# The first heads' 1x1 convolution by patch rows, in quarters of TensorE, with the first head's depthwise convolution two steps behind it

## The chip, the core and the metric

The kernel runs on one core of one Trainium2 chip. The metric is the device time of one execution in microseconds (us), the median of several runs. Engines: TensorE (matrix products; in the profile PE, its weight loads PEld), VectorE (DVE), ScalarE (ACT), GpSimd (POOL) and SyncE (SP), which issues most DMAs.

## What is computed

The input x has 48 channels of 256x256 in float32. Layer 0 is an attention over image patches, layer 1 a product along width, height and channels in windows of 64; both act on a group norm (16 groups of three channels) and are added to their input.

```python
# layer 0, on g = group norm of x
qkv = einsum('bchw,oc->bohw', g, w_qkv)          # 1x1 convolution, 48 -> 144 channels
qkv = dwconv3x3(qkv, w_dw)                       # depthwise 3x3, zero border
q, k, v = split(qkv, 3)                          # then patches of 4x4, 8 heads of 96 x 4096
q, k = l2norm(q), l2norm(k)                      # over the 96 values of a patch and head
attn = softmax(einsum('bhcn,bhcm->bhnm', q, k) * temperature)
out = fold(einsum('bhcn,bhnm->bhcm', v, attn))
x = x + einsum('bchw,oc->bohw', out, w_proj)
# layer 1, on the group norm of the new x
x = x + sum_t einsum('bchw,wW,hH,cC->bCHW', windows of 64, Ws[t], Hs[t], Cs[t])
```

## The kernel before

**Reading x (L403 to L423).** `xr` holds the whole image, its upper and lower 128 rows as two halves of 48 partitions (96 in all). Ten parts per half are loaded, one half through SyncE's queue, the other through ScalarE's; VectorE takes statistics of every two rows (L422), and `group_stats` turns them into a mean and a factor per channel. These go into the weights: `wq` (heads 0 and 1, a block per half) and `wr` (heads 2 to 7) are scaled (L425, L426), and `bias` is made of the means. The weights themselves are 35 small loads on GpSimd's queue (L87 to L112, `dwt` the last 21 of them); the row of zeros `zr` (L407), which borders the DRAM copies, is cleared by GpSimd too.

**The 1x1 convolution of heads 0 and 1 (L469 to L478, `pointwise`).** For each two rows of both halves one matmul (96 partitions in, 72 out, 512 columns) fills one of four PSUM buffers, which ScalarE (L156) and VectorE (L154) empty in turn into `ot0`, four buffers of eight rows. Each is stored into the DRAM tensor `t1[0]`. Heads 2 to 7 follow during the attention, in `Strip`, two rows at a time with half of the array for each half of the image (L177).

**The depthwise convolution (`Depthwise`).** A head's 64 patch rows (four pixel rows each) lie in seven chunks of nine. Step r treats patch row r of all seven chunks at once: 3 x 7 x 6 = 126 partitions (q, k and v; chunk; channel), each with a `pad` of six rows of 258 pixels, the four of the patch row and one on either side. Ten steps cover the head (the tenth is patch row 63). `load` reads `pad` from DRAM with three DMAs; the nine taps are either `first` on ScalarE and eight `tap`s on VectorE (L228), or 18 matmuls against diagonal matrices on TensorE (`taps_on_tensor`, L217). Then follow `square` (ScalarE, L239), `reduce` (VectorE, L243), `norm` (TensorE, L247, adds up over a head's channels), `root` and `scale` (VectorE), `patches` (ScalarE, L279, sorts pixels by patch), `high` and `low` (the split into two parts, L285 and L289), and three stores into `qkv`.

**Head 0 (`depthwise_first`).** Steps 0, 2, 4, 6, 8 and 9 have their taps on TensorE, 1, 3, 5 and 7 on VectorE. The order of TensorE's instructions is that of the program text (`manual_schedule`): taps of step 0, taps of step 2, norms of steps 0 and 1, taps of step 4, norms of 2 and 3, and so on. The other engines' instructions, and the DMA queues', are put in order by the framework's planner, which goes by the program text as far as an instruction is ready by its own costs; each engine then runs its list strictly in order. Every load of a `pad` waits for the stores of the rows that it reads.

**After that** a branch on the temperature (L494, a barrier between all engines; its body does not run here), then the keys are loaded and the attention over eight heads starts, during which the depthwise convolutions of the next head run step by step. Projection and layer 1 end the kernel.

## Time and profile before

| what | us |
|---|---|
| median of 3 runs (lowest, highest) | 3679.08 (3667.85, 3684.79) |
| profiled execution | 3676.93 |
| its span, first to last instruction | 3674.8 |
| TensorE busy in the span | 3466.3 |
| VectorE, ScalarE, GpSimd busy | 2138.7, 1872.6, 541.8 |
| last statistics of x end | 68.97 |
| first, last matmul of the 1x1 convolution | 73.8, 132.5 |
| first taps on TensorE | 147.26 |
| last norm of head 0 | 249.9 |
| queries of head 0 are loaded from | 267.6 |
| attention's logits run without waiting from | 287.2 |

Times in the profile count from the first instruction. "Busy" is the time in which an engine executes an instruction; a float32 matmul leaves two records of half its work each. "PEclk" is the clock that TensorE was granted as a share of the full one, and "DMA share" the busy share of the core's 16 DMA engines. In a timeline a line gives start, length, engine, line of the kernel, operation, what is written from what is read, the count, and in brackets the idle time before it with what ended that.

### The profile page before, as it was taken

Reading aid. Unit: us, or ns where it says so; the run is one execution under the profiler, and the core shown is the slowest. Engines: PE = TensorE matmul, PEld = TensorE weight load, DVE = VectorE, ACT = ScalarE, POOL = GpSimd, SP = SyncE. Lnnn points to the kernel's source line nnn. Section 1 sums busy time; section 2 is a strip of 40 time slices with the busy share of each in tenths; the row PEclk is TensorE's granted clock in tenths of the full one; section 3 lists DMA queues with packets and bytes.
Section 4 is the critical chain, followed back from the end, with each engine's and each line's share of the span. In section 5 each row is a group of like instructions: output and inputs, shape, how many; then the busy total and the mean of one; then the engine's idle time right before and its main releaser. Section 6 shows DMA issues by size and latency. Waiting matters only on the chain.

```text
span 3674.8 us, 100335 instructions
## 1 busy us (share of the span) xinstructions
PE 3466.3 (94%) x44252; PEld 2908.2 (79%) x44252; DVE 2138.7 (58%) x3514; ACT 1872.6 (51%) x2747; POOL 541.8 (15%) x628
## 2 busy tenths in 40 slices
PE   2869999999999999999999999999999999965998
PEld 1337777888989888888899988888899888833776
DVE  5454674179628962895389439934993222267654
ACT  0235676566646654665466556655664444400332
POOL 2030111012211211121112112211221100010011
PEclk9989999999999999999999999999999999976999
DMA  7455666533323332333233323332333220089774
GB/s 161 154 131 151 172 173 167 159 96 93 92 70 84 97 93 80 81 93 86 80 81 93 94 76 86 87 93 71 94 85 87 65 53 19 15 213 234 120 137 93
DMA packets 275299, 386.49 MB, mean 105 GB/s; under 512 B 77298, under 2 KB 211810, under 8 KB 270920
## 3 DMA queue, kind: packets, MB, share of 16 engines
q1 hardware_dynamic: 235942, 264.95, 27.4%
q0 software_dynamic: 35424, 106.40, 12.7%
q10 hardware_dynamic: 3490, 8.64, 1.1%
q8 instruction: 350, 5.73, 0.7%
q14 instruction: 93, 0.76, 0.1%
HBM read 234.76 MB, written 144.90 MB: 103 GB/s over the span
## 4 chain that ended last, share of the span: by engine, by line
PE 83%; DMA 4%; DVE 3%; issue 1%; SPq 1%; ACT 1%; POOL 0%; POOLq 0%; ACTq 0%; DVEq 0%
PE big L337 37%; PE big L601 36%; PE pb L889 4%; PE pa L867 2%; PE pc L906 2%; DMA pxt<-in_x_dram 1%; DVE acc L228 1%; PE big L177 1%; PE pt L618 1%; PE pn L247 1%; PE pst L555 1%; DMA pad<-t 0%; DVE xt L790 0%; DMA kt<-qkv 0%; DMA x1s<-pxt 0%
## 5 line engine op out<-in xcount | busy, mean ns | idle before, releaser
L572 ACT ACTIVATE e<-big,nmx 128x1024 f32<-128x1024 f32 x1024 | 1143.7, 1117 | 880.8 <-PE big L337 620.4
L337 PE MATMUL big<-kt,qt 128*128 128x512 f32 x6144 | 1439.1, 393 | 30.8 <-DMA qt<-qkv 22.1
L601 PEld LDWEIGHTS big<-vn,e 128*64 128x64 f32 x32768 | 1358.6, 137 | 57.3 <-ACT e L572 30.6
L601 PE MATMUL big<-vn,e 128*64 128x96 f32 x32768 | 1388.9, 247 | 6.1 <-DVE oacc L612 2.8
L337 PEld LDWEIGHTS big<-kt,qt 128*128 128x128 f32 x6144 | 1147.8, 189 | 278.4 <-issue 28.4
L612 DVE TENSOR_TENSOR oacc<-big,oacc 128x768 f32<-128x768 f32 x480 | 453.4, 954 | 714.5 <-PE big L601 714.5
L228 DVE SCALAR_TENSOR_TENSOR acc<-pad,dwt,acc 126x1024 f32<-126x1024 f32 x592 | 765.6, 1293 | 39.5 <-DMA pad<-t 19.1
L295 POOL DMA_DIRECT2D qkv<-o x72 | 52.7, 733 | 1245.1 <-ACT o L279 1245.1
L585 DVE TENSOR_REDUCE zt<-zs 128x1 f32<-128x4 f32 x256 | 38.5, 150 | 336.6 <-ACT e L572 336.6
L289 POOL TENSOR_TENSOR ol<-o,oh 126x1024 fp32r<-126x1024 f32 x78 | 184.7, 2367 | 310.4 <-DVE ss L243 237.9
L572 ACT ACTIVATION_READ_ACCUMULATOR e<-big,nmx 128x1 f32 x1024 | 196.4, 192 | 0.0
L896 ACT COPY lyt<-pb 128x512 f32<-128x512 f32 x144 | 84.3, 586 | 199.5 <-PE pb L889 199.5
L874 DVE TENSOR_TENSOR lzt<-pa,cbias 128x864 f32<-128x864 f32 (+1 forms) x88 | 137.0, 1628 | 82.7 <-PE pa L867 82.7
L279 ACT COPY o<-acc 126x1024 f32<-126x1024 f32 x74 | 158.5, 2142 | 0.0
L889 PEld LDWEIGHTS pb<-wsb,lzt 128*64 128x64 f32 x2304 | 125.5, 138 | 27.6 <-issue 17.9
L623 POOL DMA_DIRECT2D os__70<-oo x128 | 65.0, 514 | 534.5 <-ACT oo L621 533.8
L889 PE MATMUL pb<-wsb,lzt 128*64 128x128 f32 x2304 | 141.4, 279 | 1.2 <-DVE lzt L874 1.2
L783 PE MATMUL pps<-pot,wp 96*96 96x512 f32 x128 | 75.9, 760 | 58.0 <-DMA pot<-os__70 47.7
L239 ACT ACTIVATE sq<-acc 126x1024 f32<-126x1024 f32 x74 | 78.3, 1058 | 100.7 <-DVE acc L228 100.7
L180 ACT ACTIVATE ot<-big,bias 108x1024 f32<-108x1024 f32 x64 | 68.1, 1110 | 113.4 <-PE big L177 70.5
L209 ACT ACTIVATE acc<-pad,dwt 126x1024 f32<-126x1024 f32 x74 | 84.1, 1136 | 79.4 <-DMA pad<-t 79.4
L243 DVE TENSOR_REDUCE ss<-sq 126x64 f32<-126x1024 f32 x80 | 97.4, 1219 | 25.6 <-ACT sq L239 25.6
(127 smaller groups left out, 1902.3 us busy)
## 6 DMA issues: line engine op xcount, KB each, us to landing
pad<-t SPq DMA_DIRECT2D x238, 254.0 KB
t<-ot SPq DMA_DIRECT2D x128, 217.7 KB
qkv<-ol POOLq DMA_DIRECT2D x78, 336.0 KB, 6.4
qkv<-oh POOLq DMA_DIRECT2D x70, 336.0 KB, 5.6
qt<-qkv SPq DMA_DIRECT2D x176, 96.0 KB
xs<-in_x_dram SPq DMA_DIRECT2D x128, 96.0 KB
os__70<-oo POOLq DMA_DIRECT2D x128, 96.0 KB, 2.1
pot<-os__70 SPq DMA_DIRECT2D x16, 768.0 KB
```

The source lines that it names most:

```text
L209: nc.scalar.mul(self.acc, self.pad[:, 0:KS, 0:W], dwt[:, self.h, 0:1])
L228: nc.vector.scalar_tensor_tensor(self.acc, self.pad[:, dy : dy + KS, dx : dx + W], dwt[:, self.h, tap : tap + 1], self.acc, ALU.mult, ALU.add,
L243: nc.vector.tensor_reduce(self.ss, self.sq.rearrange("p a (x b) -> p x a b", b=KS), AX.XY, ALU.add)
L279: nc.scalar.copy(self.o.rearrange("p (a b) x -> p a b x", a=KS), self.acc.rearrange("p a (x b) -> p a b x", b=KS))
L289: eng.tensor_sub(self.ol, self.o, self.oh.bitcast(F32))
L337: nc.tensor.matmul(ps[:, i, :], lhsT=qt[:, r, q0 : q0 + 128], rhs=kts[2 * j + i][:, r // 2, :], start=(r == 0), stop=(r == 2),)
L572: nc.scalar.activation(e[:, j * 1024 : (j + 1) * 1024], ps.rearrange("p a b -> p (a b)"), AF.Exp, bias=nmx[:, b : b + 1], accum_out=zs[:, ...
L601: nc.tensor.matmul(ps[p : p + 64, j // 4, j % 4 * HD : (j % 4 + 1) * HD], lhsT=e[:, mb * 128 + p : mb * 128 + p + 64], rhs=vn, start=(i == 0),
L612: nc.vector.tensor_add(oaccs[h, k], ps[:, :, : 4 * HD], oaccs[h, k])
L874: nc.vector.tensor_tensor(zv[:, :, y0 : y0 + n, :], pa[:, :, : n * T3 * C].rearrange("p s (y k) -> p s y k", y=n), cbias.rearrange("p (u v ...
L889: nc.tensor.matmul(pb[s * WS : (s + 1) * WS, i, :], lhsT=zts[u][:, t * C + c + i, :], rhs=wsb[:, t, :], start=True, stop=True,)
L896: nc.scalar.copy(yt[:, t, :], pb.rearrange("p i x -> p (i x)"))
```

## The change

The 1x1 convolution of heads 0 and 1 no longer goes down the image but by patch rows: `pointwise(r)` makes patch row r of all seven chunks (eight for r = 0). The halves of x move to partitions 0 to 47 and 64 to 111 of `xr`, and ScalarE writes zeros into partitions 32 to 63 ahead of each part's loads, since the statistics run over all 112. `wq` is 64 columns wide for each half. Four matmuls (two halves, two chunks) go to the four quarters of TensorE and fill one PSUM buffer of two banks, of which there is one; ScalarE empties it. `ot0` has two buffers. A patch row goes into a DRAM tensor of its own, `ts[r]`, in seven or eight stores.

`pointwise` is a generator that stops after each group of four matmuls. The first three patch rows are made at once; the other six patch rows, 24 groups, are taken one by one after every second tap on TensorE. The depthwise steps go in the order 1 to 8, 0, 9, in five rounds of two: the first of a round on TensorE, the second on VectorE, and the norms of both follow in the same round. `load` reads the four rows of a patch row and the two bordering rows with one DMA each, for heads 0 and 1. `pad` has four buffers instead of eight, `o` and `ss` two instead of four, `sq`, `oh` and `ol` one. The accumulators of TensorE's taps have two PSUM buffers instead of three.

```diff
-    t1 = [dram.tile([(h1 - h0) * HC, TR, W + 2], F32, name=f"t1_{h0}") for h0, h1 in GROUPS]
+    t1 = dram.tile([M1, TR, W + 2], F32, name="t1")
+    ts = [dram.tile([H0 * 3, CH + 2, 6, KS, W + 2], F32, name=f"ts{r}") for r in range(CR)]
...
-    wq = const.tile([P2, 2 * M0], F32, name="wq")
+    wq = const.tile([64 + C, 64], F32, name="wq")
...
-            o = s * M0 + h * HC if h < H0 else (h - H0) * HC
+            o = h * HC if h < H0 else (h - H0) * HC
...
-                out=(wq[r] if h < H0 else wr[0:C])[:, o : o + HC].rearrange("c (z e) -> c z e", z=3),
+                out=(wq[s * 64 : s * 64 + C] if h < H0 else wr[0:C])[:, o : o + HC].rearrange("c (z e) -> c z e", z=3),
...
-    def pointwise(ps, dst, xs, on_vector=False):
-        nc.tensor.matmul(ps[: 2 * M0], lhsT=wq, rhs=xs.rearrange("p a b -> p (a b)"), start=True, stop=True)
-        src = ps[: 2 * M0].rearrange("p (a b) -> p a b", a=2)
-        dst = dst[:, :, 1 : W + 1]
-        if on_vector:
-            nc.vector.tensor_scalar_add(dst, src, bias[: 2 * M0, 0:1])
-        else:
-            nc.scalar.activation(dst, src, AF.Identity, bias=bias[: 2 * M0, 0:1])
+    def pointwise(r):
+        js = [[], []]
+        for j in range(CH + (r == 0)):
+            js[(j * CR + r) * KS // HALF].append(j)
+        for g in range(2):
+            ot = xnp.tile([128, 2, KS, W + 2], F32, name="ot0", bufs=2)
+            nc.gpsimd.memset(ot[:, :, :, 0:1], 0.0)
+            nc.gpsimd.memset(ot[:, :, :, W + 1 : W + 2], 0.0)
+            for d in range(2):
+                ps = pw.tile([128, 2, 512], F32, name="pw")
+                for a in range(2):
+                    for s in range(2):
+                        j = js[s][min(2 * g + a, len(js[s]) - 1)]
+                        y = (j * CR + r) * KS - s * HALF + 2 * d
+                        nc.tensor.matmul(
+                            ps[a * 64 : (a + 1) * 64, s, :],
+                            lhsT=wq[s * 64 : s * 64 + C],
+                            rhs=xr[s * 64 : s * 64 + C, y : y + 2, :].rearrange("p a b -> p (a b)"),
+                            start=True,
+                            stop=True,
+                        )
+                nc.scalar.activation(
+                    ot[:, :, 2 * d : 2 * d + 2, 1 : W + 1],
+                    ps.rearrange("p s (a b) -> p s a b", a=2),
+                    AF.Identity,
+                    bias=bias[:, 0:1],
+                )
+                yield
+            for s in range(2):
+                for a in range(2):
+                    if 2 * g + a < len(js[s]):
+                        nc.sync.dma_start(
+                            out=ts[r][:, js[s][2 * g + a] + 1].rearrange("q c y x -> q c (y x)"),
+                            in_=ot[a * 64 : a * 64 + M0, s].rearrange("p y x -> p (y x)"),
+                        )
...
-            self.pool, self.bufs = (pool, 4) if pool else (cv, 1)
+            self.pool, self.bufs = (pool, 2) if pool else (cv, 1)
...
-            g = [i for i, (h0, h1) in enumerate(GROUPS) if h0 <= self.h < h1][0]
-            c0 = (self.h - GROUPS[g][0]) * HC
             self.pad = self.pool.tile([NP1, KS + 2, W + 2], F32, name="pad", bufs=2 * self.bufs)
-            rows = t1[g][c0 : c0 + HC, self.r * KS : self.r * KS + CH * CR * KS, :]
-            rows = rows.rearrange("(z c) (j y) x -> z j c y x", z=3, j=CH)[:, :, :, : KS + 2, :]
-            for z in range(3):
-                engs[z % len(engs)].dma_start(out=self.pad[z * NZ : (z + 1) * NZ], in_=rows[z])
+            if self.h >= H0:
+                c0 = (self.h - H0) * HC
+                rows = t1[c0 : c0 + HC, self.r * KS : self.r * KS + CH * CR * KS, :]
+                rows = rows.rearrange("(z c) (j y) x -> z j c y x", z=3, j=CH)[:, :, :, : KS + 2, :]
+                for z in range(3):
+                    engs[z % len(engs)].dma_start(out=self.pad[z * NZ : (z + 1) * NZ], in_=rows[z])
+                return
+            for i, (k, y0, n, ys) in enumerate(((0, 1, KS, 0), (-1, 0, 1, KS - 1), (1, KS + 1, 1, 0))):
+                j, r = divmod(self.r + k, CR)
+                src = ts[r][self.h * 3 : (self.h + 1) * 3, j + 1 : j + 1 + CH, :, ys : ys + n, :]
+                engs[i % len(engs)].dma_start(
+                    out=self.pad[:, y0 : y0 + n, :].rearrange("p y x -> p (y x)"),
+                    in_=src.rearrange("z j c y x -> z (j c) (y x)"),
+                )
...
+        def tap_on_tensor(self, diag, ps, n):
...
+            nc.tensor.matmul(
+                ps[:, i, :],
+                lhsT=diag[:, tap, :],
+                rhs=self.pad[:, y : y + 2, dx : dx + W],
+                start=(tap == 0),
+                stop=(tap == 8),
+            )
...
         def square(self):
-            self.sq = self.pool.tile([NP1, KS, W], F32, name="sq", tag="t4" if self.bufs == 1 else "sq", bufs=self.bufs)
+            self.sq = self.pool.tile([NP1, KS, W], F32, name="sq", tag="t4" if self.bufs == 1 else "sq", bufs=1)
...
         def high(self):
-            self.oh = self.pool.tile([NP1, KK, PX], F32R, name="oh", bufs=self.bufs)
+            self.oh = self.pool.tile([NP1, KK, PX], F32R, name="oh", bufs=1)
...
         def low(self, eng=nc.vector):
-            self.ol = self.pool.tile([NP1, KK, PX], F32R, name="ol", tag="t4", bufs=self.bufs)
+            self.ol = self.pool.tile([NP1, KK, PX], F32R, name="ol", tag="t4", bufs=1)
...
-    def depthwise_first():
-        with tc.tile_pool(name="dg", bufs=1) as dg, tc.tile_pool(name="dps", bufs=3, space=PSUM) as dps:
...
-            rows = [Depthwise(0, r, dg) for r in range(CR + 1)]
-            on_tensor = [r for r in range(CR + 1) if r % 2 == 0 or r == CR]
...
-            for d in rows[:2]:
-                d.load((nc.sync, nc.scalar))
-            for d in rows[2:6]:
-                d.load()
-            with tc.manual_schedule(engines={mybir.EngineType.PE}):
-                taps(0)
-                for i in range(0, CR + 1, 2):
-                    if i + 1 not in on_tensor:
-                        taps(i + 1)
-                    taps(min(i + 2, CR))
-                    for d in rows[i + 6 : i + 8]:
-                        d.load()
-                    for d in rows[i : i + 2]:
-                        late = d.r >= CR - 1
-                        d.square()
-                        d.reduce()
-                        d.norm()
-                        d.root(on_scalar=True)
-                        d.scale()
-                        d.patches()
-                        d.high()
-                        d.store((0,), nc.sync)
-                        d.low(nc.vector if late else nc.gpsimd)
-                        d.store((1,), nc.sync if late else nc.gpsimd)
-                        d.store((2,), nc.gpsimd if late else nc.sync)
-    with tc.tile_pool(name="xn", bufs=1) as xnp, tc.tile_pool(name="cst", bufs=1) as cst, tc.tile_pool(
-        name="nps", bufs=2, space=PSUM
-    ) as nps, tc.tile_pool(name="pw", bufs=4, space=PSUM) as pw:
-        zr = cst.tile([128, W + 2], F32, name="zr")
+    def depthwise_first(dg, dps):
+        diag = dg.tile([NP1, 9, NP1], F32, name="diag")
+        for t in range(9):
+            nc.gpsimd.tensor_scalar_mul(diag[:, t, :], ident[:NP1, :NP1], dwt[:, 0, t : t + 1])
+        order = list(range(1, CR)) + [0, CR]
+        rows = [Depthwise(0, r, dg) for r in order]
+        rounds = (None for r in range(3, CR) for _ in pointwise(r))
+        with tc.manual_schedule(engines={mybir.EngineType.PE}):
+            for r in range(3):
+                for _ in pointwise(r):
+                    pass
+            rows[0].load()
+            for i in range(0, CR + 1, 2):
+                d, e = rows[i : i + 2]
+                ps = dps.tile([NP1, 2, 512], F32, name="dps")
+                for n in range(18):
+                    d.tap_on_tensor(diag, ps, n)
+                    if n % 2:
+                        next(rounds, None)
+                e.load()
+                if i + 2 <= CR:
+                    rows[i + 2].load()
+                e.first()
+                for t in range(1, 9):
+                    e.tap(t)
+                for f in (d, e):
+                    f.square()
+                    f.reduce()
+                    f.norm()
+                    f.root(on_scalar=True)
+                    f.scale()
+                    f.patches()
+                    f.high()
+                    f.store((0,), nc.sync)
+                    f.low(nc.vector if i == CR - 1 else nc.gpsimd)
+                    f.store((1,), nc.sync if i == CR - 1 else nc.gpsimd)
+                    f.store((2,), nc.gpsimd)
...
+        zr = pre.tile([128, W + 2], F32, name="zr")
...
-        xr = xnp.tile([P2, HALF, W], F32, name="xr")
-        parts = [16] * 7 + [8, 4, 4]
-        st0 = cst.tile([P2, HALF * W // 512, 6], F32, name="st0")
+        for y in (0, H + 1):
+            nc.gpsimd.dma_start(out=t1[:, y, :], in_=zr[:M1])
+        for r, j, y in ((CR - 1, 0, KS - 1), (1, CH + 1, 0)):
+            nc.gpsimd.dma_start(out=ts[r][:, j, :, y, :], in_=zr[:M0])
+        g0 = pre.tile([64 + C, 64 + C], F32, name="g0")
+        nc.vector.memset(g0, 0.0)
+        for i in (0, 64):
+            for j in (0, 64):
+                nc.gpsimd.dma_start(out=g0[i : i + C, j : j + C], in_=gmat[0:C, 0:C])
+        xr = xnp.tile([64 + C, HALF, W], F32, name="xr")
+        parts = [8, 8] + [16] * 6 + [8, 4, 4]
+        st0 = pre.tile([64 + C, HALF * W // 512, 6], F32, name="st0")
         for i, LR in enumerate(parts):
             j = sum(parts[:i])
+            nc.scalar.mul(
+                xr[32:64, j : j + LR, :].rearrange("p a b -> p (a b)"), zr[32:64, 0:1].to_broadcast([32, LR * W]), 0.0
+            )
             for s in range(2):
                 eng = nc.sync if s == 0 else nc.scalar
                 eng.dma_start(
-                    out=xr[s * C : (s + 1) * C, j : j + LR, :], in_=xc[:, s * HALF + j : s * HALF + j + LR, :]
+                    out=xr[s * 64 : s * 64 + C, j : j + LR, :], in_=xc[:, s * HALF + j : s * HALF + j + LR, :]
                 )
             for i in range(0, LR, 2):
...
-        group_stats(st0, mean0, rstd0, cst, nps)
...
+        pb = nps.tile([128, 1], F32, name="pb0", tag="pstat")
+        for s in range(2):
+            r = slice(s * 64, s * 64 + C)
+            nc.tensor.matmul(pb[s * 64 : (s + 1) * 64], lhsT=wq[r], rhs=mean0[r], start=True, stop=True)
+        nc.vector.tensor_scalar_mul(bias[:, 0:1], pb, -1.0)
...
-        OR = 8
-        for y in range(0, HALF, OR):
-            ot = xnp.tile([2 * M0, OR, W + 2], F32, name="ot0", bufs=4)
-            nc.gpsimd.memset(ot[:, :, 0:1], 0.0)
-            nc.gpsimd.memset(ot[:, :, W + 1 : W + 2], 0.0)
-            for i in range(0, OR, 2):
-                ps = pw.tile([128, 512], F32, name="pw")
-                pointwise(ps, ot[:, i : i + 2, :], xr[:, y + i : y + i + 2, :], on_vector=(i // 2 % 2 == 1))
-            for s, rows in enumerate(both_halves(t1[0], y, OR, base=1)):
-                nc.sync.dma_start(out=rows, in_=ot[s * M0 : (s + 1) * M0])
-    attention = ExitStack()
+        first.close()
+        one = attention.enter_context(tc.tile_pool(name="one", bufs=2, space=PSUM))
+        with tc.tile_pool(name="dg", bufs=1) as dg, tc.tile_pool(name="dps", bufs=2, space=PSUM) as dps, tc.tile_pool(
+            name="pw", bufs=1, space=PSUM
+        ) as pw:
+            depthwise_first(dg, dps)
```

## Prediction

> **What bounds the kernel now.** I read the page first (TensorE busy 94% of the span, ScalarE and VectorE about half), then the stretches of the part that the change touches, everything before the first logits at 287 us; the 3390 us behind it run code that the change leaves alone. The stage table (busy time of each engine, granted clock, DMA share):
>
> ```profile
> core 0: us, PE busy (x) PEld busy (x) DVE busy (x) ACT busy (x) POOL busy (x), PEclk, DMA share, GB/s
> 0.00:73.80 73.80, 5.98 (x26) 5.43 (x27) 45.50 (x96) 1.49 (x2) 23.20 (x54) 1.00 0.86 173
> 73.80:134.00 60.20, 58.73 (x132) 19.20 (x131) 24.22 (x34) 21.85 (x32) 2.46 (x26) 1.00 0.51 153
> 134.00:147.30 13.30, 0.04 (x1) 0.07 (x1) 0.00 (x0) 0.00 (x0) 5.55 (x15) 0.54 0.38 131
> 147.30:250.30 103.00, 98.05 (x236) 43.88 (x236) 73.80 (x76) 36.42 (x39) 27.07 (x16) 0.98 0.49 132
> 250.30:267.10 16.80, 0.01 (x1) 0.00 (x0) 6.13 (x8) 6.05 (x7) 1.45 (x2) 0.52 0.53 108
> ```
>
> Five steps in series: x is read (to 73.8), the 1x1 convolution fills TensorE (to 134), a DRAM round trip leaves it idle for 13 us, the depthwise convolution of head 0 fills it again for 103 us, and a tail of 17 us ends in the branch. The change wants the second and third to lie beside the fourth. What paces the first is in the timelines of POOL and VectorE:
>
> ```profile
> 4.07 2.28 POOL L102 DMA_DIRECT2D wr<-in_w_qkvT_dram  x4
> 11.97 0.58 POOL L102 DMA_DIRECT2D wr<-in_w_qkvT_dram  x1 [5.62 <-DMA tb<-in_temp_dram]
> ...
> 32.78 0.52 POOL L106 DMA_DIRECT2D wp<-in_w_projT_dram  x1 [4.27 <-DMA wr<-in_w_qkvT_dram]
> ...
> 65.00 6.12 POOL L112 DMA_DIRECT2D dwt<-in_w_dw_dram  x11 [0.49 <-DMA dwt<-in_w_dw_dram]
> 71.11 0.33 POOL L407 MEMSET zr<- 128x258 f32 x1
> ```
> ```profile
> 50.84 4.84 DVE L422 BATCH_NORM_STATS2 st<-xr 96x6 f32<-96x512 f32 x8 [2.80 <-DMA xr<-in_x_dram]
> 59.38 9.59 DVE L422 BATCH_NORM_STATS2 st<-xr 96x6 f32<-96x512 f32 x16 [3.71 <-DMA xr<-in_x_dram]
> ```
>
> POOL issues 35 small loads in program order; from the ninth on each waits for the landing of the one eight before it, some 3.6 us apiece while x saturates the DMA engines, 0.56 us apiece once it doesn't. Only then, at 71.1, does it clear `zr`. VectorE's 64 statistics (0.605 us each, 38.7 in sum) hide behind the load except for the last.
>
> In the depthwise stage the order of TensorE is written by hand, two rows of taps ahead of the norms:
>
> ```profile
> 147.26 33.52 PE L217 MATMUL dps<-pad,diag 126*126 126x512 f32 x72 [14.72 <-DMA pad<-t]
> 180.61 0.55 PE L247 MATMUL pn<-ss,same 126*126 126x64 f32 x4
> 181.00 15.67 PE L217 MATMUL dps<-pad,diag 126*126 126x512 f32 x36
> 196.50 0.55 PE L247 MATMUL pn<-ss,same 126*126 126x64 f32 x4
> ```
>
> The norms (L247) need the sums that VectorE makes of both rows; since TensorE does the next row's taps first, they find these ready, and nearly nothing is lost.
>
> **Part 1: reading x.** `xr` grows to 112 partitions, and ScalarE must zero partitions 32 to 63 of each part from `zr` before the lower half's transfer (which writes 32 to 47 of them) may start. `zr` still stands behind the 35 POOL loads. The upper half's transfers wait for nothing; I take them to go first on ScalarE's queue, since the list order of before lets ready work pass (VectorE clears `pick` and `row` at 1.4 us ahead of statistics written earlier). Half of x, 6.3 MB, at the 200 GB/s of this stage lasts until about 33 us. With one stream instead of two I take POOL's landings at half the distance, 1.9 us: first landing about 6.5, some 15 by 33 us, so 23 loads issued, the other 12 by 0.56: `zr` at 40. Bounds: 22 (35 x 0.58, never held up) and 45 (held up as before until 33, then 20 x 0.56). Then ScalarE clears 8 rows: 2048 elements, by its rows of 1024 elements (1.11 us) and 512 (0.68) 0.86 ns an element and 0.24 to start, so 2.0 us; 393 KB land in about 4 us; and from 46 on VectorE has all its 38.7 us still before it: 84.7 instead of 69.0. ScalarE's clearing (about 31 us in all, 3.8 per 16 rows) and the transfers (3.9 per 16 rows) keep ahead of VectorE's 4.84. **+16 us**, between 0 (`zr` by 24) and +36 (the clearing at the 2.14 us that ScalarE's strided copies out of SBUF take per 1024, 61 us in all: 40 + 61 + 5 = 106). The extra border and `gmat` loads on POOL hide behind the statistics: at 0.56 us each some 5 us, on the path only if `zr` came at the end of them.
>
> **Part 2: the first three patch rows.** 64 matmuls of the whole array (55 us) become 36 groups of four quarter matmuls. What a group costs is seen in two places of the last and middle stages:
>
> ```profile
> 3509.04 2.81 PE L906 MATMUL pc<-lyt,hsb 64*64 64x512 f32 x24
> 363.41 1.97 PE L177 MATMUL big<-xs,wr 48*108 48x512 f32 x8
> 365.60 5.50 PE L601 MATMUL big<-vn,e 128*64 128x96 f32 x128 [0.22 <-DVE oacc L612]
> ```
>
> Twelve quarter matmuls in 2.81: 0.94 a group, so the quarters do run side by side. Four half-array ones between other shapes take 1.90 start to start where 4 x 0.43 would be 1.71: 0.19 for changing shape and back; I take 1.05 a group between taps. But there is one PSUM buffer, and ScalarE alone empties it (1.11 us for 108x1024, L180): TensorE and ScalarE alternate, 0.95 + 1.1 + 0.3 of handing over = 2.35 us a group, TensorE busy 40%; at half clock it would be 1.9 + 1.4 = 3.3 us and 58%. In the projection stage 57% is found at half clock:
>
> ```profile
> 3290.00:3300.00 10.00, 5.69 (x7) 1.82 (x8) 9.97 (x11) 0.00 (x0) 1.00 (x2) 0.50 0.96 328
> ```
>
> Twelve groups: 28.2 to 39.6; I take 39.6, by that row. The Trainium skill's page "TensorE: Matmul & The Clock Gate" (HAM oscillation) ties the fall to gaps above about 3.4 us; the gaps here are about 1.4, so by that rule the clock would stay up and the sum be 11 us lower. Then the last stores must land: before, an `ot` tile's buffer came free about 5 us after its last write (memset at 90.36, tile full at about 85.4); bounds 2.0 (the border stores' landing) and 6. Then one padded row is read, three transfers of 762 KB: 8.5 us in the two undisturbed cases (138.8 to 147.3, 304.6 to 313.1); with larger pieces I take 7.5, between 5 (762 KB at 170 GB/s) and 11.3 (the longest wait for it in the chain). First tap 39.6 + 5 + 7.5 = 52 us after the weights, before 147.3 - 73.8 = 73.5: **-21.5 us**.
>
> **Part 3: five rounds of two rows.** This is where I expect the loss. Each round puts 18 taps of one row on TensorE (36 passes of 0.43, 15.4 us) with up to nine groups between them, then at once the norms of that row *and* of the round's second row, which VectorE computes. The order is by hand, so all later taps queue behind the second norm. The second row of round 0 (row 2) needs patch row 3, whose last group is the fourth of that same round. The chain from there: eviction with handing over 1.3, stores 5, row load 7.5, first tap on ScalarE 1.15, eight taps 10.3, square 1.05, sum 1.2, norm 0.4 = 27.9 us, from these rows:
>
> ```profile
> L228 DVE SCALAR_TENSOR_TENSOR acc<-pad,dwt,acc 126x1024 f32<-126x1024 f32 x40 | 57.1, 1427 | 24.7 <-DMA pad<-t 19.1 <-ACT acc L209 4.6
> L239 ACT ACTIVATE sq<-acc 126x1024 f32<-126x1024 f32 x5 | 5.2, 1049 | 2.1 <-DVE acc L228 2.1
> L243 DVE TENSOR_REDUCE ss<-sq 126x64 f32<-126x1024 f32 x11 | 13.3, 1214 | 5.8 <-ACT sq L239 5.8
> ```
>
> (Eight uncontended taps are 10.53 us in the timeline.) A pair of taps and a group is 1.72 + 1.05 = 2.77, and a round that starts after an idle stretch loses 2.5 us at half clock, as at 147 (first records 1188 ns, later 589). Round 0: 4 x 2.77 + 2.5 + 27.9 = 41.5. Round 1 waits for the third of its groups: 38.7; round 2 for its second: 35.9. Rounds 3 and 4 have all data and go by VectorE: two roots 1.9, two scalings 2.4, taps 10.3, two sums 2.4, square 1.05, and 2 us of taps stretched where POOL subtracts (single taps of 2.3 and 3.1 us at 207 to 213): 20 each. To the last norm 116 + 40 = 156 us; before, 249.9 - 147.3 = 102.6. **+53.5 us**. With stores at 2 and loads at 5 each of the three rounds and the start shrink by 5.5.
>
> **Part 4: tail.** From the last norm to the branch 17.2 us; the last row is now one of VectorE's, whose patch copy takes 2.14 instead of 1.01: **+1**. `oh`, `ol` and `sq` now have one buffer each, so a row's parts wait until those of the row before are stored (5 to 6 us, the landings of `qkv<-ol` have a median of 6.3); between two norms of a round that takes 20 us and more there is room, in the tail 0 to 6 us may show: 0, since the first row of the round is normed while the second is still on VectorE. Halo loads of head 1 in the attention stage carry the same bytes; that SP queue has slack there: 0.
>
> **Sum.** 16 - 21.5 + 53.5 + 1 = +49 us on the profiled execution's 3676.9 us (span 3674.8), 2 us below the median 3679.1: 3726. All low ends together: 0 + (28.2 + 2 + 5 - 73.5 = -38) + (53.5 - 16.5 = 37) + 1 = 0; all high ends about +84.
>
> **Rivals.** *The rows keep up (faster).* If the second row's data were there when a round starts, TensorE would set the pace: 24.8 + 24.8 + 21.7 + 2 x 20 = 111 to the last norm (+9), with the first tap at -38 and x not held up: -28, 3649. It decides if a second row's pad lands within about 10 us of the round's start; against it stands that its fourth group alone ends after 11. Chance 0.10. *A draw:* `zr` early and short transfers, 3677; 0.17. *Clearing dear:* part 1 at +36, 3746; 0.13. The forecast: 0.60.
>
> **Range and chances.** 3665 leaves out the faster case and a little of the draw; 3765 takes in nearly all high ends. Faster by over 0.5% (18 us, about what a measurement tells from no change) 0.10, within 0.17, slower 0.73.
>
> **What would show it.** Statistics ending near 85 instead of 69 and `zr` near 40; first tap some 52 us after the weights; in three rounds a gap of 8 to 15 us before a norm of L247, ended by VectorE's sum; the norms' rounds 36 to 42 us apart, then 20. I am wrong if `zr` is cleared by 24, or TensorE never waits for the sums.

## The result, and the profile after

The changed kernel takes 3856.8 us (median of 4 runs, 3851.8 to 3870.4) where the kernel before took 3677.0 beside it: a ratio of 1.049, 95% interval 1.047 to 1.051. The direction was as forecast; the size was 180 us instead of 49, and outside the range. The profiled execution's span went from 3674.8 to 3850.0 us, +175.2. The stages of the changed kernel, which answer to the first table of the prediction:

```profile
core 0: us, PE busy (x) PEld busy (x) DVE busy (x) ACT busy (x) POOL busy (x), PEclk, DMA share, GB/s
0.00:107.80 107.80, 6.06 (x28) 5.52 (x29) 46.10 (x97) 31.41 (x14) 25.84 (x55) 1.00 0.75 121
107.80:149.30 41.50, 26.15 (x102) 4.36 (x100) 0.36 (x3) 13.34 (x12) 6.04 (x18) 1.00 0.22 72
149.30:163.30 14.00, 0.00 (x0) 0.03 (x1) 0.00 (x0) 0.04 (x1) 0.29 (x4) 1.00 0.22 77
163.30:378.70 215.40, 128.24 (x391) 45.25 (x391) 85.31 (x84) 64.20 (x64) 34.73 (x44) 0.79 0.30 94
378.70:395.90 17.20, 0.65 (x2) 0.46 (x2) 6.49 (x9) 6.59 (x6) 1.72 (x8) 0.50 0.44 105
416.00:766.00 350.00, 313.59 (x3574) 250.65 (x3575) 204.29 (x339) 206.15 (x272) 45.35 (x36) 0.93 0.52 142
```

The reading of x ends 34.0 us later, the way from there to the first tap is 18.0 shorter, the rounds take 112.8 more (215.4 against 102.6), and what follows the last norm takes 46.4 more (3471.3 against 3424.9). That last loss was forecast as 1 us. The sixth line shows where it is: in the first 350 us of attention TensorE is busy 313.6 us. The same stretch of the kernel before, counted from its own first logits:

```profile
288.00:638.00 350.00, 342.27 (x4094) 275.30 (x4092) 216.09 (x373) 236.03 (x316) 50.39 (x40) 0.98 0.59 164
```

Attention's code is the same but for head 1's loads of patch rows. Yet fewer bytes move (142 GB/s against 164), and the DMA engines are less busy, not more. In the rounds, too, TensorE and VectorE wait while the DMA engines show a share of 0.30. Something holds the transfers, and it is neither their bytes nor that all DMA engines are busy.

The timeline of TensorE, the norms of the first three rounds (the matmuls between them left out; in brackets the idle time before each, and what ended it):

```profile
202.27 0.43 PE L285 MATMUL pn<-ss,same 126*126 126x64 f32 x2 [2.55 <-DVE ss L281]
212.79 0.69 PE L285 MATMUL pn<-ss,same 126*126 126x64 f32 x2 [10.09 <-DMA pad<-ts]
255.95 0.68 PE L285 MATMUL pn<-ss,same 126*126 126x64 f32 x2 [4.58 <-DVE ss L281]
258.29 0.69 PE L285 MATMUL pn<-ss,same 126*126 126x64 f32 x2 [1.66 <-DVE ss L281]
295.61 0.43 PE L285 MATMUL pn<-ss,same 126*126 126x64 f32 x2 [2.37 <-DVE ss L281]
323.71 0.68 PE L285 MATMUL pn<-ss,same 126*126 126x64 f32 x2 [27.68 <-DVE ss L281]
```

The wait that the prediction named, before the second norm of a round, is there in the first and the third (10.1 and 27.7 us), hardly in the second (1.7). And the rounds do not fall from 41 to 36 us: they take 50.0, 45.5, 65.4, 31.2 and 23.2 us. And the reading of x, in the timelines of POOL, ScalarE and VectorE:

```profile
26.95 11.76 POOL L114 DMA_DIRECT2D dwt<-in_w_dw_dram  x21
38.70 0.34 POOL L444 MEMSET zr<- 128x258 f32 x1
```
```profile
0.74 2.29 ACTq L465 DMA_DIRECT2D xr<-in_x_dram  x5
...
39.07 1.91 ACT L460 ACTIVATE xr<-zr 32x2048 f32<-32x2048 f32 x1 [34.72 <-POOL zr L444]
40.88 19.42 ACT L460 ACTIVATE xr<-zr 32x2048 f32<-32x2048 f32 x6
57.69 0.32 ACTq L465 DMA_DIRECT2D xr<-in_x_dram  x1
...
76.74 0.32 ACTq L465 DMA_DIRECT2D xr<-in_x_dram  x1
```
```profile
54.87 2.47 DVE L469 BATCH_NORM_STATS2 st<-xr 112x6 f32<-112x512 f32 x4 [38.32 <-DMA xr<-in_x_dram]
...
93.27 9.59 DVE L469 BATCH_NORM_STATS2 st<-xr 112x6 f32<-112x512 f32 x16 [0.59 <-DMA xr<-in_x_dram]
```

`zr` is cleared at 38.7 (forecast 40). But ScalarE had issued only five of the upper half's transfers by then; the others stand behind clears, up to 77 us. From 20 to 40 us the DMA engines stood at a share of 0.24, and the statistics end at 102.9, not 84.7:

```profile
20.00:40.00 20.00, 0.00 (x0) 0.00 (x0) 0.00 (x0) 0.93 (x1) 15.24 (x28) 1.00 0.24 25
```

### The profile page after: what moved, and what is told of

Same layout as the page of the kernel before. It is cut to its first block, busy times and chain, and to the rows that moved or that the text cites. A ratio compares the mean times of both kernels' runs of the same rounds, so it can differ in the third digit from the quotient of the medians.

```text
span 3850.0 us, 100643 instructions
## 1 busy us (share of the span) xinstructions
PE 3480.8 (90%) x44378; PEld 2905.8 (75%) x44378; DVE 2130.7 (55%) x3491; ACT 1924.4 (50%) x2764; POOL 551.5 (14%) x644
## 4 chain that ended last, share of the span: by engine, by line
PE 79%; DMA 5%; issue 3%; SPq 2%; DVE 1%; ACT 0%; POOL 0%; POOLq 0%; ACTq 0%; DVEq 0%
PE big L375 35%; PE big L644 34%; PE pb L932 4%; PE pa L910 2%; PE pc L949 2%; DMA xs<-in_x_dram 1%; DMA pad<-ts 1%; PE big L207 1%; DMA vt<-qkv 1%; PE pt L661 1%; DMA t<-ot 1%; DMA x1s<-pxt 1%; PE pn L285 1%; PE pst L598 1%; SPq L349 1%
## 5 line engine op out<-in xcount | busy, mean ns | idle before, releaser
L266 DVE SCALAR_TENSOR_TENSOR acc<-pad,dwt,acc 126x1024 f32<-126x1024 f32 x600 | 774.1, 1290 | 163.7 <-ACT acc L248 115.5
L210 ACT ACTIVATE ot<-big,bias 108x1024 f32<-108x1024 f32 x64 | 68.9, 1112 | 143.3 <-PE big L207 75.7
```

The lines of the kernel that those rows point to most:

```text
L266: nc.vector.scalar_tensor_tensor(self.acc, self.pad[:, dy : dy + KS, dx : dx + W], dwt[:, self.h, tap : tap + 1], self.acc, ALU.mult, ALU.add,
```

## The experiments

All are compared by the same four stretches, read from TensorE's timeline as in the table (us; "rest" is from the last norm to the end of the span).

| kernel | weights ready | to first tap | to last norm | rest | time |
|---|---|---|---|---|---|
| before | 73.8 | 73.4 | 102.6 | 3424.9 | 3677 |
| layout_alone | 76.1 | 87.9 | 130.4 | 3484.0 | 3780 |
| loads_by_z | 75.0 | 88.0 | 103.4 | 3421.8 | 3690 |
| stores_wide | 72.7 | 71.0 | 102.6 | 3426.9 | 3681 |
| narrow_before | 74.8 | 80.7 | 111.6 | 3465.8 | 3735 |
| after | 107.8 | 55.5 | 215.4 | 3471.3 | 3857 |
| zeros_early | 82.0 | 55.4 | 214.1 | 3473.1 | 3826 |
| norms_later | 108.7 | 55.4 | 195.4 | 3487.1 | 3848 |
| five_rows_ahead | 108.1 | 69.2 | 180.0 | 3478.3 | 3837 |
| change_by_z | 109.3 | 50.2 | 171.5 | 3431.8 | 3763 |
| change_by_z_zeros | 87.5 | 50.2 | 172.9 | 3419.5 | 3732 |
| by_z_norms_later | 85.8 | 50.3 | 164.7 | 3426.9 | 3730 |
| psum_halves | 90.9 | 47.2 | 173.3 | 3429.8 | 3743 |
| halves_norms_later | 85.7 | 46.2 | 157.6 | 3438.6 | 3730 |
| all_mended | 107.3 | 46.9 | 157.5 | 3434.4 | 3750 |
| all_rows_first | 88.5 | 119.2 | 125.2 | 3426.5 | 3761 |

The changed kernel, change_by_z and all_mended ran four times, stores_wide ten times; every other time of a version is one run. The stretches are compared rather than the times where little is at stake: the medians of the kernel before beside the different groups of runs are 3675 to 3688 us, and the rest of like kernels differs by some 6 us either way.

**First round: one part of the change at a time.** The layout by itself, in the kernel before:

```diff
+ ts = [dram.tile([H0 * 3, CH + 2, 6, KS, W + 2], F32, ...) for r in range(CR)]
- nc.sync.dma_start(out=rows, in_=ot[s * M0 : (s + 1) * M0])             # 8 rows
+ nc.sync.dma_start(out=ts[r][:, j + 1]..., in_=ot[s * M0 ..., k : k + KS]...)  # 4 rows
- engs[z % len(engs)].dma_start(out=self.pad[z * NZ : (z + 1) * NZ], in_=rows[z])
+ engs[i % len(engs)].dma_start(out=self.pad[:, y0 : y0 + n, :]..., in_=src.rearrange("z j c y x -> z (j c) (y x)"))
```

> The kernel before, with only the DRAM layout of the change for heads 0 and 1: patch rows in ts, stored in 64 pieces instead of 32, each padded row read by one DMA for its four rows and one for each bordering row. Theory: the 47 us that the attention of head 0 lost come from these loads, which share SyncE's queue with the strips, queries and values; so about 3720 us, the part before the first unhindered logits within 15 us of 287 us, the part behind it 40 to 50 us longer than 3388. Rival: they come from something else of the change (buffers placed elsewhere, a different start); then 3670 to 3690 us and the part behind it within 5 us of 3388.

It took 3780.1 us, 92 more than the kernel before beside it (3688.1), far beyond what either theory had given it. In the spans it is 103: 2 in the reading, 14.5 in the way to the first tap, 28 in the depthwise stage, 59 behind it. Half of the whole loss is in this part.

Early zeros:

```diff
-        nc.gpsimd.memset(zr, 0.0)
+        nc.vector.memset(zr, 0.0)
```

> The changed kernel, with the row of zeros cleared by VectorE at the start instead of by GpSimd behind its 35 small loads. Theory: the late zeros cost the whole of the 34 us in reading x; statistics end at 69 to 72 us instead of 102.9, and the kernel takes about 3822 us (-32). Rival: ScalarE's clearing itself, some 31 us with the upper half's DMA issues between its steps, or the transfers into two separated blocks of partitions hold x up; statistics end after 80 us, 3830 to 3850 us.

3826.4 us, 30 less than after (25 in the span); the weights came at 82.0 instead of 107.8 and nothing else moved. So the late zeros cost 25 to 30 us; the weights still come 8 us later than in the kernel before (14 on the mean of the five later runs with early zeros).

The norms of a round behind the next round's taps, as the kernel before has them:

```diff
+                if i:
+                    finish(i - 2)
-                for f in (d, e):
-                    f.square()
...
+            finish(CR - 1)
```

> The changed kernel, with the norms of a round written after the taps and groups of the next round, as the kernel before has them. Theory: TensorE's waits at the norms (66 us in all) go, but the first three rounds are then held by the padded row of the next round, whose last patch row is made, stored and read within the round: periods of about 38, 36 and 33 us instead of 50, 45 and 65; about 3800 us (-55, at least -35). Rival: the interleaved groups (one PSUM buffer, two ot buffers, changes of shape) hold the rounds; then no more than -15.

3848.5 us, 8 less (3 in the span) where the theory of the prediction gave 55. The rounds are 20 us shorter, but the last rows then come out later, and most of it is given back behind the last norm. TensorE's order held 20 us of the rounds, but not the time.

Five patch rows ahead of the first tap instead of three (`range(3)` to `range(5)`):

> The changed kernel, with five patch rows instead of three made before the first taps, so that each round's second row and the next round's first row are complete a round earlier. Theory: 8 more groups at 3.3 us make the first tap 26 us later, but the rounds fall to 20 to 28 us each, together about 125 instead of 215 us; about 3790 us (-64). Rival: the rounds stay above 35 us since something other than late data sets them (the norms in TensorE's order alone, ScalarE's list); then 3840 to 3880 us.

3837.3 us, 19 less, against 64 expected: the rounds lose 35, the way to the first tap grows by 14.

**The new theory.** What the windows of layout_alone show, beside one of the kernel before:

```profile
155.00:200.00 45.00, 33.95 (x72) 14.29 (x72) 10.94 (x9) 3.21 (x3) 2.06 (x4) 0.84 0.20 75
```
```profile
140.00:160.00 20.00, 12.74 (x24) 5.55 (x25) 7.38 (x6) 1.15 (x1) 4.43 (x8) 0.70 0.43 168
```

Both stretches load patch rows and little else. In the kernel before the DMA engines' share is 0.43, that is 6.9 of 16, at 24 GB/s each; the DRAM side of a load there runs over 7 chunks first. With the new layout it is 0.20, 3.2 engines at 23 GB/s each, and the DRAM side runs over q, k, v first: 3. The stores of the new layout run over 6 first; in layout_alone, beside the 1x1 convolution, the share is 0.37, 5.9 engines:

```profile
82.00:147.00 65.00, 53.58 (x123) 17.40 (x121) 23.06 (x31) 20.88 (x31) 1.72 (x24) 0.93 0.37 141
```

Each transfer seems to be served by only as many engines as its outermost dimension has entries. The Trainium skill states such a rule (DMA: Bandwidth & Descriptors, section on why a DMA increments its semaphore by 16): the largest number up to 16 that divides the slowest dimension of both sides. Two runs put it to the test from both sides: loads_by_z keeps bytes and places of layout_alone and cuts the one large load in three, narrow_before keeps those of the kernel before and cuts its loads to 3 and 4 chunks.

```diff
-                engs[i % len(engs)].dma_start(out=..., in_=src.rearrange("z j c y x -> z (j c) (y x)"))
+                for z in range(3):     # main part: 42 x 4128 B each
+                    engs[z % len(engs)].dma_start(out=out[z * NZ : (z + 1) * NZ], in_=src[z])
```

> The kernel layout_alone (the kernel before with head 0's and head 1's rows kept as patch rows, and nothing else of the change), with one edit: the main part of a patch row's load, 126 partitions of 4128 B in one DMA whose DRAM side is 3 x 42 x 4128 B, is issued as three DMAs of 42 x 4128 B. The bytes, their places in DRAM and the two halo loads stay. Theory N (narrow DMAs): a DMA is served by only as many DMA engines as the outermost dimension of its access patterns allows. In layout_alone from 155 to 200 us, while these loads ran, the DMA engines' mean share was 0.20 at 75 GB/s, 3.2 engines of 16 at 23 GB/s each, for an outermost dimension of 3; in the kernel before from 140 to 160 us 0.43 at 168 GB/s, 6.9 engines, for one of 7. By N the main part is no longer what a round waits for, the halos (127 KB each at 75 GB/s, 1.7 us) run beside it: first tap to last norm near before's 102.6 us (layout_alone 130.4), the rest after the first logits near 3388 us (layout_alone 3446), the time 3700 us (3685 to 3720). Theory P (place: patch rows lie badly in DRAM, or pieces of 4 KB and 1 KB are dear): 3770 to 3790 us as in layout_alone. The Trainium skill, DMA: Bandwidth & Descriptors, section on why a DMA increments its semaphore by 16, states that the largest number up to 16 that divides the slowest dimension of both sides is used: 3 before this edit and 14 after it.

```diff
+                for a, b in ((0, 3), (3, CH)):
-                engs[z % len(engs)].dma_start(out=self.pad[z * NZ : (z + 1) * NZ], in_=rows[z])
+                    engs[z % len(engs)].dma_start(out=self.pad[z * NZ + a * 6 : z * NZ + b * 6], in_=rows[z][a:b])
```

> The kernel before, with its old layout, each of the three DMAs of a patch row's load cut along the chunks into one of 3 chunks and one of 4 (six DMAs, outermost dimensions 3 and 4 in place of 7). Bytes, places and pieces are the same. Theory N (a DMA is served by as many engines as its outermost dimension has entries, and each engine moves some 24 GB/s, which is 168 GB/s by 6.9 engines in the kernel before from 140 to 160 us): if the narrow DMAs share the same few engines, the load of 762 KB takes 8 to 10 us where it took 4.5, and the kernel loses as layout_alone did: 3740 us (3715 to 3790). Theory P (place and pieces): no change but three more issues of 0.73 us a load on SyncE, which has slack: 3680 to 3700 us.

loads_by_z: 3690.0 us, 13 over the kernel before beside it where layout_alone was 92; the depthwise stage is back at 103.4 us and the rest at 3421.8. narrow_before: 3735.0 us, 58 more than the kernel before, from nothing but a cut. Its loads run at a share of 0.24, 3.8 engines, not 7:

```profile
155.00:200.00 45.00, 44.54 (x101) 19.68 (x102) 26.79 (x26) 10.68 (x11) 3.92 (x3) 0.93 0.24 92
```

So the two pieces of a cut load do not take 3 and 4 engines side by side: they share engines or follow one another, which the share can't tell apart. The same section has it that they share them (the lowest-numbered engines are taken). The outermost dimension is shown as the cause: loads_by_z has more and wider DMAs and is faster, narrow_before more and narrower ones and is slower. The rule of division agrees with 3, 6 and 7. For 42 it gives 14, which no stretch shows: while change_by_z loads its first patch row, from 155 to 157 us, the share is 0.65, some 10 engines, at 196 GB/s.

**The change without its narrow main loads**, with the same cut (its loads of bordering rows, 3 wide, and its stores, 6 wide, stay):

> The kernel after, with the main part of each patch row's load as three DMAs of 42 x 4128 B, one for each of q, k and v, in place of one whose outermost dimension is 3. Nothing else differs. Theory N: what the narrow loads cost goes: 47 us in head 0's attention, and of the 112.8 us that the five rounds lost some 40 to 60; the stores (6 x 6 x 4128 B, 141 GB/s at a share of 0.37 in layout_alone) and the late zeros stay. From 3857 us to 3760 us (3735 to 3785). Theory Q (the rounds are held by the in-order lists of ScalarE, SyncE and TensorE, and the loads only stand at their end): the attention's 47 us return, of the rounds less than 15: 3795 to 3812 us. Theory P (place and pieces): 3840 to 3860 us.

3763.0 us in 4 runs, ratio to the kernel before 1.0235 (1.0216 to 1.0255): 94 us of the 180 are the narrow loads. In the spans it is 87: 44 in the rounds, 40 behind them, 5 ahead of the first tap, and weights that come 1.5 later. Attention's first 350 us read as in the kernel before again:

```profile
371.00:721.00 350.00, 341.61 (x4074) 274.90 (x4073) 216.26 (x373) 235.15 (x316) 50.43 (x40) 0.98 0.60 162
```

Who had waited there tells how the narrow loads did their harm. The rows of waits of after and of change_by_z (in total, times, longest), in these windows:

```profile
PE pst L598 <- DMA vt<-qkv: 16.8, 5, 5.8
PE big L207 <- DMA xs<-in_x_dram: 11.8, 4, 7.9
```
```profile
PE big L207 <- DMA xs<-in_x_dram: 1.6, 1, 1.6
...
PE pst L601 <- DMA vt<-qkv: 0.2, 1, 0.2
```

Not the depthwise rows themselves but the values and the input strips, whose own transfers are unchanged, had come late: they were held up by the narrow ones, be it in SyncE's queue or on the engines that they share; no run separates the two.

> As change_by_z, and zr is cleared by VectorE instead of GpSimd (as in zeros_early, which alone took the kernel after from 3857 to 3826 us). If the two causes add, 30 us under change_by_z: 3730 us (3705 to 3755) by theory N, 3765 to 3782 by theory Q, 3810 to 3830 by theory P. If the gain of the early zeros is taken back where the loads wait, less than 15 us under change_by_z.

3731.8 us: the two causes add, and 55 us over the kernel before are left, near the 49 of the forecast.

**What the 55 are.** The norms' order, the gaps of the quarters, or the data? Four runs on top of change_by_z_zeros (the norms' edit is that of norms_later; all keep the narrow stores and bordering rows):

> As change_by_z_zeros (the change with loads by q, k and v and zr cleared by VectorE, 3732 us), and the norms of a round follow one round later in TensorE's order, behind the next round's taps, as in norms_later. In change_by_z_zeros TensorE waits 38.0 us in all at the ten norms (row of the norm's matmul, idle until the sum of squares), and round starts lie 38.7, 48.3, 34.7 and 28.4 us apart. Theory R (with the loads wide, the order of TensorE holds the rounds, as the prediction said): most of the 38 us go, less some 10 us for the last pair's norms behind the last taps: 3704 us (3692 to 3715). Theory L (the in-order lists of ScalarE, where the first tap of a row stands ahead of the squares, hold the rounds): as in norms_later, where it was worth 8 us: 3715 to 3735.

3729.5 us: the rounds lose 8, but the first logits follow the last norm after 30.9 us instead of 21.5 and start at 331.7 us of the span instead of 332.0. Nothing is gained.

```diff
-                ps = pw.tile([128, 2, 512], F32, name="pw")        # one buffer, one eviction
+                for s in range(2):
+                    ps = pw.tile([128, 512], F32, name="pw")       # two buffers
```

> As change_by_z_zeros, but a group of the 1x1 convolution (8 records of TensorE, one PSUM tile of two banks, one eviction of 128 x 1024 by ScalarE, 1.11 us) becomes two halves with a bank of their own: TensorE fills one while ScalarE empties the other. In change_by_z_zeros a group takes 3.3 us: 1.98 us for 8 records at half clock and a gap of 1.24 to 1.36 us for the eviction. Theory C (the gap is what keeps the clock at half): without it the clock comes up, and a group takes the two evictions of 128 x 512, about 0.68 us each as in the kernel before: 1.4 to 1.6 us; the 12 groups ahead of the first tap take 18 us where they took 40, and the rounds, which wait for norms, gain up to 8: 3706 us (3698 to 3716), weights to first tap 30 us where it was 50. Theory H (the clock stays at half, whatever the gap): 1.98 us a group, 24 us for the 12: 3712 to 3720. Theory S (the halves cost ScalarE more than they save in its list): 3725 or more.

3743.2 us, so no gain, and a surprise in TensorE's timeline:

```profile
95.97 2.55 PE L166 MATMUL pw<-xr,wq 48*64 48x512 f32 x8 [0.76 <-ACT ot L173]
98.73 2.55 PE L166 MATMUL pw<-xr,wq 48*64 48x512 f32 x8 [0.21 <-ACT ot L173]
101.51 2.55 PE L166 MATMUL pw<-xr,wq 48*64 48x512 f32 x8 [0.23 <-ACT ot L173]
```

TensorE is now busy 2.55 of 2.76 us, and still a group doesn't fall to the 1.4 to 1.6 us of theory C: its records stay at 1057 to 1112 ns, those of half the clock (below). It gains some 0.4 us a group, 5 us in the lead, of which 3 reach the first tap.

> As psum_halves, and with the norms one round later as in by_z_norms_later. If the two add (28 and 26 us): 3675 us (3655 to 3692), about the time before. Then a round's steps are TensorE's own work: 18 taps of two records and their groups. If they overlap (both take the same wait out of the rounds): no better than the better of the two, less 5 us: 3695 to 3705.

3730.1 us: the rounds take 157.6, and the rest is 19 us longer than in change_by_z_zeros, so that what the rounds gain is given back.

```diff
+        for j, LR in zip(at, parts):
+            nc.scalar.dma_start(out=xr[64 : 64 + C, j : j + LR, :], in_=xc[...])
+        for i, (j, LR) in enumerate(zip(at, parts)):
+            [nc.vector, nc.gpsimd][i % 2].memset(xr[32:64, j : j + LR, :], 0.0)
```

> As halves_norms_later, with two more edits. The upper half's loads of xr all stand first in ScalarE's list, and the clears of xr's 16 unused partitions are taken from ScalarE and shared by VectorE and GpSimd; in the 12 groups ahead of the first tap VectorE empties every second half. In change_by_z_zeros the weights are ready at 87.5 us, in the kernel before at 73.8, with 152 GB/s in the first 20 us where the kernel before had 187. Expected: weights at 74 to 80 us (12 us earlier), the 12 groups some 5 us shorter: 17 us less than halves_norms_later, 3658 us (3640 to 3680), so a little faster than the kernel before or equal to it. If GpSimd's clears are as slow as its clear of zr (which ended at 38.7 us in the kernel after), the lower half's loads wait for them, and the weights come later than 87.5: 3690 or more.

3749.9 us, ratio 1.0209 (1.0182 to 1.0236), a miss: GpSimd's clears stood behind its 35 small loads, as `zr` had, and ran from 68.8 to 81.8 us; the weights came at 107.3.

```profile
57.07 7.22 POOL L114 DMA_DIRECT2D dwt<-in_w_dw_dram  x13 [0.47 <-DMA dwt<-in_w_dw_dram]
...
68.76 13.04 POOL L468 MEMSET xr<- 32x2048 f32 x5
```

Then all nine patch rows ahead of the first tap (`range(3)` to `range(CR)`, no groups in the rounds):

> As change_by_z_zeros (3732 us; weights 87.5, first tap 137.7, last norm 310.9), with all nine patch rows of the 1x1 convolution ahead of the first tap in place of three, so 36 groups at 3.3 us: 119 us ahead of it and nothing of it in the rounds. Theory D (the rounds are held by data: their rows are made one or two rounds earlier and come by store and load): with all rows in DRAM the rounds take what the kernel before needs, 103 to 115 us where they took 173; first tap at 216, last norm at 320 to 332, time 3741 to 3753 us. Theory L (the order of the norms and the in-order lists hold the rounds whatever the data): the rounds lose only the groups themselves, 24 groups of 1.1 us: 145 us, last norm at 361, 3780 us or more.

3761.1 us, between the theories. The rounds shrink from 172.9 to 125.2 us. Of the 70 us that they take over the kernel before, 48 go with the rows that are made inside them (24 groups of 1.1 us are 26; the other 21 are waits that went with them), and 23 stay with all rows in DRAM. TensorE's waits for the sums in these rounds still come to 33.9 us, in each round beside 17.2 us of taps.

**The layout, cleared.** loads_by_z kept 13 us over the kernel before, all ahead of the first tap, where its 20 last stores (6 x 6 pieces) leave SyncE at 1.06 us each:

```profile
127.81 21.13 SPq L494 DMA_DIRECT2D ts<-ot  x20
```

stores_wide makes them 36 wide and loads the bordering rows, too, by q, k and v:

```diff
- ts = [dram.tile([H0 * 3, CH + 2, 6, KS, W + 2], ...)]     # store: 6 x 6 x 4128 B
+ ts = [dram.tile([H0 * 3 * 6, CH + 2, KS, W + 2], ...)]    # store: 36 x 4128 B
```

> As loads_by_z (the kernel before with patch rows, loads by q, k and v; 3690 us), with the patch rows of a channel one after the other in DRAM, so that a store of 36 partitions x 4128 B has an outermost dimension of 36 in place of 6, and a load one of 7 in place of 42; the halos too are loaded by q, k and v (nine DMAs a load). In loads_by_z the last 20 stores leave SyncE from 127.8 to 148.9 us, 1.06 us each, and TensorE waits 27.1 us for the first loads, where the kernel before waits 14.7: by theory N (as many engines as the outermost dimension allows) the stores were the bound there at 138 GB/s and a share of 0.37, which is 6 engines of 16. Wide stores then give the 12 us back: 3678 us (3670 to 3688), the kernel before's time within its scatter, so the layout costs nothing by itself. If more issues on SyncE (0.75 us each, nine a load) take their place: 3690 to 3705.

3680.6 us in 10 runs against 3682.1: ratio 1.0002 (0.9989 to 1.0015). Patch rows in DRAM cost nothing where every transfer is at least 7 wide. No version here beats the kernel before; this one equals it. The change itself with wide stores, on top of change_by_z_zeros, was not run, so how much of the 55 us its 6-wide stores and 3-wide bordering rows make is open; in the kernel before they made some 13 (loads_by_z against stores_wide).

## Why the prediction was wrong

The span was missed by 126 us: 59 in part 3, 45 in part 4, 18 in part 1 and 3.5 in part 2. The price of a patch row's load runs through the first two.

**Part 4, the failing step.** "Halo loads of head 1 in the attention stage carry the same bytes; that SP queue has slack there: 0" was measured at +46.4 in the rest of the span, and loads_by_z and change_by_z take it away without touching a byte. The same omission sits in part 3, where a row's load was 7.5 us "with larger pieces". By 762 KB at the 75 GB/s that layout_alone showed it is 10.4 us with all engines of those transfers free, and the first load of after held TensorE 15.1 us, that of change_by_z 9.8. The profile of before had the hint: at 0.43 and 168 GB/s its loads were already limited by something while the load of x ran at 0.99 and 203. I read the 170 GB/s as the speed of a load; it was that of some seven engines, and the diff's access pattern starts with a 3. In time: 94 us, more than the 84 of all high ends together.

**Part 1, +34 instead of +16.** `zr` at 40 held (38.7), though by luck in part: with the transfers at a standstill, the last 21 small loads left at 0.56 us each from 27 us on, where the sum had 12 left at 33. "The upper half's transfers go first" did not: five did, and the others stood among the clears in ScalarE's list, so that from 20 to 40 us the transfers stood nearly still and the rest of x had to land after 41. The end was paced by the load, not by VectorE's 38.7 us. With early zeros the weights come at 82 to 91 us, still 8 to 17 after the kernel before's, though ScalarE's clears are over at 38 us (change_by_z_zeros): what holds that remainder is open.

**Part 2, -18 instead of -21.5, held.** Twelve groups at half clock took 3.3 us each, the row-based value to the tenth:

```profile
113.39 1.98 PE L166 MATMUL pw<-xr,wq 48*64 48x512 f32 x8 [1.28 <-ACT ot L173]
116.60 1.99 PE L166 MATMUL pw<-xr,wq 48*64 48x512 f32 x8 [1.23 <-ACT ot L173]
119.90 1.99 PE L166 MATMUL pw<-xr,wq 48*64 48x512 f32 x8 [1.31 <-ACT ot L173]
```

From the last eviction to the first tap it was 14.0 us instead of 12.5; TensorE's idle stretch there, 15.1 us in after, fell to 9.8 with wide loads. That it was half the clock is read from the records' length, not from the clock column: the trace's first record of the clock is at 166.6 us, and the 1.00 of the table ahead of it stands for no record. Behind it, the same eight records take 1.09 us where the profile grants the full clock and 1.99 us where it grants half (176.1 us), and those ahead of it are as long as the latter:

```profile
166.83 1.09 PE L166 MATMUL pw<-xr,wq 48*64 48x512 f32 x8
...
176.12 1.99 PE L166 MATMUL pw<-xr,wq 48*64 48x512 f32 x8 [6.29 <-ACT ot L173]
```

So the clock did not fall between the groups, it never rose. In all_rows_first all 36 groups, 119 us, ran at half, and the first clock record comes 4 us after the first tap. The matmuls of 96 x 72 in the kernel before, without a gap, started at half too (records of 1061 ns) and were at the full clock (592 ns) from 80.4 us on, 6.6 us after the first of them. The Trainium skill's "TensorE: Matmul & The Clock Gate" (HAM oscillation) ties half clock to gaps above 3.4 us; here no gap was above 1.4, in psum_halves none above 0.8, and 12 groups stayed slow. The measurement decides: row, not rule. The reason why I took half clock, a busy share of 58%, is not shown either: at some 90% busy, in psum_halves, it stayed. Why is open.

**Part 3, +112.8 instead of +53.5.** 44 of the excess are the narrow loads. Without them the stage is +70, and the mechanism holds in part. That rows made inside the rounds hold them up is shown (all_rows_first, -48, of which 26 are the groups themselves). But the gap of 8 to 15 us before a norm, forecast for three rounds, shows in one of them once the loads are wide (3.9, 10.8 and 1.7 us before the second norms of change_by_z_zeros). And TensorE's hand-written order, which the prediction called the reason for the loss, is worth next to nothing on the time (norms_later 8 us, by_z_norms_later 2): where norms follow later, the last rows come later, and head 0's first logits wait for them. The rounds were under-sized by some 17 us: in change_by_z_zeros they take 38.7, 48.3, 34.7, 28.4 and 22.8 us where the sum had 41.5, 38.7, 35.9, 20 and 20, so the sum was 10 short for the second and 11 for the two that go by VectorE. The sum left out that the other lists are in order too. In after, ScalarE waits 51.0 us in all for `pad` at the first tap of a row, with squares and evictions queued behind it, and evictions wait for stores in turn; how much of the 17 us this makes was not separated:

```profile
PE pn L285 <- DVE ss L281: 56.1, 9, 27.7
...
ACT acc L248 <- DMA pad<-ts: 51.0, 5, 24.6
...
DVE acc L266 <- DMA pad<-ts: 32.3, 3, 16.6
...
ACT ot L173 <- DMA ts<-ot: 14.6, 3, 8.4
```

The sign was right, then, for part of the reason of part 3. With the narrow loads mended and the zeros early, change_by_z_zeros stands at +55 beside the forecast's +49, stretch by stretch +13.7 for +16, -23.2 for -21.5, +70.3 for +53.5, and -5 in the rest, within its scatter. That the two sums lie so close is luck in part: +16 was worked out for a `zr` cleared at 40, which this run clears at the start, and the 17 us that part 3 lacks are partly made up by the other three parts.

## What to carry to other kernels

Before costing a transfer, read the outermost dimension of both of its sides: equal bytes in larger pieces moved at less than half the rate here with 3 in place of 7 (75 GB/s against 168), and the narrow transfers also held up others. The sign in a profile is waiting on a DMA while the DMA share is low; a share times 16 tells how many engines are busy on average. When a new operand has to be cleared or loaded, place it by what stands ahead of it in that engine's list (`zr`, and once more the clears of all_mended, stood behind 35 small loads). Before blaming one engine's order, take the data wait away. And where a clock column has no record yet, read the clock from the length of like matmuls.

## What was not expected of the hardware

- DMA engines by outermost dimension: 3 gave a share of 0.20 at 75 GB/s, 6 (stores beside the 1x1 convolution) gave 0.37 at 141, 7 gave 0.43 at 168; loads cut into 3 and 4 gave 0.24 at 92.
- Quarter matmuls (48 x 64) alone stayed at half the clock (1.98 us per 8 records, against 1.09 between taps of 126 x 126) with gaps of 1.3 us, for 40 us on end and in all_rows_first for 119, and with gaps of some 0.2 to 0.5 as well (2.55 us busy of 2.76). That a quarter counts as little activity is a guess.
- A clear of 32 x 2048 elements took GpSimd 2.6 us each (13.04 for 5) and ScalarE 1.9.
